# Folding a layer norm's scale and shift into the next weights, moving two norms to ScalarE, and laying the instruction order anew, in a two-layer graph transformer

## The chip, the cores and the metric

The kernel runs on one core of a Trainium2 chip. The metric is the device time of one execution in microseconds (us), the median of three runs. Inputs are 32 graphs of 512 nodes with 256 features in float32, and one 512 x 512 integer adjacency matrix for each graph.

The engines that matter here are TensorE (PE, matrix products into PSUM), its weight loads (PEld), VectorE (DVE), ScalarE (ACT), GpSimd (POOL) and the DMA queues, which are issued by SyncE (SP) and by POOL. Each engine takes its instructions strictly in the order in which the program gives them to it, and an instruction that waits for a semaphore holds up all that follow on its engine.

## The reference, cut to what matters

Each graph goes through two layers of masked attention with residuals and layer norms. `_layernorm` without arguments has no scale and shift. There are four norms for a graph; the kernel numbers them 1 to 4.

```python
def _layernorm(x, g, b):
    m = mean(x); v = mean(square(x - m))
    return (x - m) * rsqrt(v + EPS) * g + b

# layer 0
allowed = (adj > 0) | (adj.T > 0) | eye
q, k, v = split(x @ Wqkv.T + bqkv)                    # 8 heads of 32
attn    = softmax(where(allowed, q @ k.T / sqrt(32), -inf))
x1      = _layernorm(x + (attn @ v) @ Wo.T + bo, ln1_g, ln1_b)              # norm 1
ff      = relu(x1 @ W1.T + b1) @ W2.T + b2                                  # 256 -> 1024 -> 256
y       = _layernorm(x1 + ff, ln2_g, ln2_b)                                 # norm 2
x2      = _layernorm(x + y)                                                 # norm 3
# layer 1: the same attention with other weights and mask (adj != 0), no MLP
out     = _layernorm(x2 + attention(x2) @ Wo.T + bo)                        # norm 4
```

## The kernel before

All of it is a software pipeline over graphs. A class `Graph` has one small method for each step, and `period(a, b, c, d, e)` lists the steps of five graphs that are at different stages, in the order in which each engine shall execute them. `opening` (the first graphs), 29 calls of `period`, and `closing` (the last three graphs) make the whole program. This list is the schedule.

The steps that the change touches, and those that a reader needs to follow the prediction:

```python
def statistics(self, y, n, i):                    # mean and variance of one 128-row chunk
    ...
    nc.vector.bn_stats(st, y)                     # L428
    nc.vector.bn_aggr(self.mv[n][:, i, :], st)    # L429

def root(self, n, a, b):                          # rs = (var + EPS) ** -0.5, chunks a to b
    nc.gpsimd.tensor_scalar(rs, self.mv[n][:, a:b, 1:2], EPS, None, ALU.add)      # L434
    nc.gpsimd.tensor_tensor(rs, rs, neg_half[:, a:b, None], ALU.pow)              # L435

def affine(self, dst, y, g, b, n, i):             # two passes of VectorE
    nc.vector.scalar_tensor_tensor(c, y, self.mean(n, i), g, ALU.subtract, ALU.mult)             # L442
    nc.vector.scalar_tensor_tensor(dst, c, self.rs[n][:, i, :], b, ALU.mult, ALU.add)            # L443

def out0(self, i):                                # residual and statistics of norm 1
    self.residual_statistics(self.po[i // 2][:, i % 2, :], self.x1, 1, i)        # L447, 428, 429
def norm1(self, i):
    self.affine(self.x1[:, i, :], self.y.pop(i), g1, be1, 1, i)
def residual1(self):                              # x1 += b2, by an accumulating DMA
    add_row(self.x1, b2)
def norm2(self, i): ...                           # affine with g2, then statistics of norm 3
def norm3(self, i):
    nc.vector.tensor_scalar(self.x2[:, i, :], self.y.pop(i), mean, rs, ALU.subtract, ALU.mult)   # L516
def offset(self, a, b):                           # -mean * rs, for norm 4 only
    nc.vector.scalar_tensor_tensor(self.ms[:, a:b, :], self.mv[4][:, a:b, 0:1], -1.0, ...)       # L525
def norm4(self, i):
    nc.scalar.activation(self.x2[:, i, :], self.y.pop(i), AF.Identity, bias=..., scale=...)      # L530

def scores(self, layer, k):                       # one of 8 beats of a layer: 4 heads x 128 keys
    s = ps_s.tile([P, HPC, N], F32, ...)          # the only buffer of this pool (bufs=1)
    for j in range(HPC):
        nc.tensor.matmul(s[:, j, :], kT..., qT..., ...)        # L343, four row tiles of 32
    nc.scalar.activation(p, s, AF.Exp, scale=SCALE)            # L347
def masked(self, layer, k):                       # p *= mask, 128 x 2048            L352
def product(self, k):                             # acc += v.T @ p, column tiles of 32   L360
def pair(self, k):                                # p[k] += p[k+1], by a DMA of POOL     L375
def fold(self, dst, a, b):                        # p[dst] = p[a] + p[b], VectorE        L379
def sums(self, k, hg, ...):                       # ones.T @ p: softmax denominators     L400
def divide(self, hg):                             # transpose, reciprocal, transpose, multiply
def transpose(self, src, h):                      # TensorE transposes of 2 chunks       L301
def once(self):  value_bias(0)                    # first graph only: bv @ Wo + bo, needs Wo of layer 0
def once1(self): value_bias(1)                    # the same for layer 1
# project (L459), query_key (L330), value (L313), hidden (L479) and mlp (L500) are plain matmuls;
# with transpose, sums and value_bias they share ps_d, a ring of 3 PSUM buffers.
```

The loads before the loop, on the SP queue, and the last store:

```python
first.load()                                      # x of graph 0
for dst, src in resident[:5]: ...                 # Wqkv (q, k), bq, bk, Wqkv (v), bv
first.cast(); first.entries(); first.again()      # adjacency to bf16, its transposes, x again
for dst, src in resident[5:7]: ...                # Wo of layer 0, bo
second.load(); second.again()
for dst, src in resident[7:]: ...                 # W1, b1, W2, ..., Wo of layer 1, bo
...
c.store(0, 2)                                     # closing: rows of the first two chunks
c.root(4, 2, 4); c.offset(2, 4); c.norm4(2); c.norm4(3)
c.store(2, 4)
```

Of the kernel before, what the change touches and what calls it, by code (L numbers as in the profile page):

```python
# [27 lines left out]
def kernel(ctx: ExitStack, tc: tile.TileContext, t: dict, out: bass.AP):  # L28
# [15 lines left out]
    P = 128  # L44
# [49 lines left out]
    w_t, src = resident.pop()  # L94
    resident.append((w_t[:, :, : 2 * D], src[:, :, : 2 * D]))
# [8 lines left out]
    resident.insert(3, (w_t[:, :, 2 * D :], src[:, :, 2 * D :]))  # L104
# [4 lines left out]
    g1, be1 = spread("L0_gnn_ln1_g"), spread("L0_gnn_ln1_b")  # L109
    g2, be2 = spread("L0_gnn_ln2_g"), spread("L0_gnn_ln2_b")  # L110
# [11 lines left out]
    bov = [const.tile([P, D], F32, name=f"bov_{layer}") for layer in range(2)]  # L122

# [29 lines left out]
    def plain(pools: ExitStack):  # L153
# [16 lines left out]

        def add_row(dst, row):
            nc.gpsimd.dma_start(out=dst, in_=row[:, None, :].to_broadcast([P, NQ, D]), accum_op=ALU.add)
# [7 lines left out]
        class Graph:  # L180


            def __init__(self, b):
                self.b = b
                self.mv, self.rs, self.pf, self.total = {}, {}, {}, {}
# [45 lines left out]
            def once(self):  # L231

                if self.b == 0:
                    value_bias(0)

# [231 lines left out]
            def norm1(self, i):  # L467
                self.affine(self.x1[:, i, :], self.y.pop(i), g1, be1, 1, i)
# [20 lines left out]
            def residual1(self):  # L489
                add_row(self.x1, b2)  # L490
# [23 lines left out]
            def norm3(self, i):  # L514
                mean, rs = self.mean(3, i), self.rs[3][:, i, :]
                nc.vector.tensor_scalar(self.x2[:, i, :], self.y.pop(i), mean, rs, ALU.subtract, ALU.mult)  # L516
# [4 lines left out]
            def offset(self, a, b):  # L521

                if a == 0:
                    self.ms = small.tile([P, NQ, 1], F32, tag="ms", name=f"ms_{self.b}", bufs=2)
                nc.vector.scalar_tensor_tensor(  # L525
                    self.ms[:, a:b, :], self.mv[4][:, a:b, 0:1], -1.0, self.rs[4][:, a:b, :], ALU.mult, ALU.mult
                )

            def norm4(self, i):
                nc.scalar.activation(  # L530
                    self.x2[:, i, :], self.y.pop(i), AF.Identity, bias=self.ms[:, i, :], scale=self.rs[4][:, i, :]
                )

            def store(self, a=0, b=NQ):
                nc.sync.dma_start(
                    out=out[self.b].rearrange("(c p) d -> p c d", p=P)[:, a:b, :], in_=self.x2[:, a:b, :]
                )
# [4 lines left out]
        def period(a, b, c, d, e):  # L542
# [3 lines left out]
            c.scores(0, 0)  # L546
            a.fold(3, 6, 7)
            b.hidden(1, 0)
            b.hidden(1, 2)
            c.scores(0, 1)  # L550
            c.masked(0, 0)
            b.hidden(1, 4)
            b.hidden(1, 6)
            c.masked(0, 1)
            a.fold(3, 3, 4)
# [859 lines left out]
```

## Time and profile before

| | value |
|---|---|
| time, median of 3 runs | 3093.09 us (3091.61 to 3094.91) |
| busy PE, DVE, ACT, POOL, share of the span | 99%, 86%, 55%, 34% |
| mean granted TensorE clock | 0.996 |
| opening, up to the first scores of the first period | 186.7 us |
| 29 periods | 2751.1 us, 94.86 each |
| closing | 155.4 us |
| DMA traffic | 406.54 MB, 131 GB/s |

The profile comes from one execution. Its page gives busy time by engine, the span in 40 slices, the chain of work that ended last, and groups of instructions by source line with their mean duration. Answers of the trace add views of a window: the timeline of an engine, who waited for whom, and busy times by stretch. "L343" is a line of the kernel file. A count such as x16 in the trace is twice the number of matmul calls in the code, because a float32 matmul appears as two instructions. The bounds of opening, periods and closing were read from the timeline of PE: the scores that begin the first period start at 186.66 us and those that begin the closing at 2937.74 us.

### The profile page before, as it was taken

How to read it: one execution, taken by the hardware profiler on the slowest of the kernel's cores; microseconds unless marked ns; L12 is line 12 of the kernel's file. 1: busy time of each engine (PE TensorE's matmuls, PEld its weight loads, DVE VectorE, ACT ScalarE, POOL GpSimd, SP SyncE). 2: the span in 40 equal slices, each digit the busy share in tenths (PEclk: the TensorE clock that was granted, in tenths of full speed). 3: DMA queues.
4: the chain of work that ended last, by engine and by line, in shares of the span. 5: the costliest groups of instructions: out<-in, count | busy, mean ns of one | idle time of the engine just before them, and what ended most of it. 6: DMA issues, size and time to landing. Idle time of an engine off the chain costs nothing.

```text
span 3093.1 us, 44243 instructions
## 1 busy us (share of the span) xinstructions
PE 3052.6 (99%) x17218; PEld 1732.7 (56%) x17218; DVE 2648.2 (86%) x3458; ACT 1706.4 (55%) x1983; POOL 1039.8 (34%) x1254
## 2 busy tenths in 40 slices
PE   6999999999999999999999999999999999999998
PEld 2656555555555555555655555555556555555554
DVE  4798898888898888988888988889888899888887
ACT  4455655555565556655555655556555655555554
POOL 1232334332343323333333433233333334332332
PEclk8999999999999999999999999999999999999999
DMA  8776776666676666776676766668666777666542
GB/s 192 134 138 115 140 143 140 123 130 130 137 151 123 133 124 136 147 139 125 122 138 137 146 120 132 123 137 155 129 133 114 141 144 140 121 131 128 116 88 63
DMA packets 341352, 406.54 MB, mean 131 GB/s; under 512 B 149648, under 2 KB 315920, under 8 KB 316432
## 3 DMA queue, kind: packets, MB, share of 16 engines
q0 software_dynamic: 95824, 282.09, 50.8%
q1 hardware_dynamic: 245312, 121.56, 15.9%
q8 instruction: 137, 2.24, 0.3%
q14 instruction: 79, 0.65, 0.1%
HBM read 89.01 MB, written 33.55 MB: 40 GB/s over the span
## 4 chain that ended last, share of the span: by engine, by line
PE 92%; DVE 3%; DMA 2%; SPq 1%; issue 1%; ACT 1%; POOL 0%; POOLq 0%; DVEq 0%; ACTq 0%
PE psS L343 17%; PE psH L479 15%; PE psF L500 14%; PE psA L360 14%; PE psQK_None L330 10%; PE psV L313 7%; PE psO L459 7%; PE psR L400 4%; PE psQK L330 3%; PE psT L301 2%; DVE p L352 1%; DMA p<-p 1%; DMA v<-in_x_dram 1%; DMA s_L_gnn_ln_g<-in_L_gnn_ln_g_dram 0%; ACT p L347 0%
## 5 line engine op out<-in xcount | busy, mean ns | idle before, releaser
L347 ACT ACTIVATE p<-psS 128x2048 f32<-128x2048 f32 x512 | 961.8, 1879 | 652.9 <-PE psS L343 647.4
L352 DVE TENSOR_TENSOR p<-p,m 128x2048 f32<-128x2048 f32 x512 | 1155.3, 2279 | 30.3 <-ACT p L347 30.3
L434 POOL TENSOR_SCALAR rs<-mv 128x2 f32<-128x2 f32 (+1 forms) x320 | 321.7, 1005 | 935.6 <-DVE mv L429 933.6
L343 PE MATMUL psS<-qT,kT 32*128 32x512 f32 x4096 | 585.6, 641 | 8.0 <-ACT p L347 6.2
L360 PE MATMUL psA<-p,v 128*32 128x512 f32 x4096 | 491.9, 598 | 0.9 <-ACT cT L370 0.7
L500 PE MATMUL psF<-w_L_gnn_W,hT 128*128 128x256 f32 x2048 | 469.1, 383 | 0.0
L479 PE MATMUL psH<-xT,w_L_gnn_W 128*128 128x256 f32 x2048 | 467.4, 384 | 0.0
L500 PEld LDWEIGHTS psF<-w_L_gnn_W,hT 128*128 128x128 f32 x2048 | 384.5, 190 | 124.2 <-issue 77.6
L479 PEld LDWEIGHTS psH<-xT,w_L_gnn_W 128*128 128x128 f32 x2048 | 382.2, 190 | 117.5 <-issue 44.7
L379 DVE TENSOR_TENSOR p<-p,p 128x2048 f32<-128x2048 f32 x189 | 429.2, 2286 | 2.6 <-DMA p<-p 2.4
L343 PEld LDWEIGHTS psS<-qT,kT 32*128 32x128 f32 x4096 | 160.6, 184 | 305.2 <-issue 114.3
L435 POOL TENSOR_TENSOR rs<-rs,neg_half 128x2 f32<-128x2 f32 (+1 forms) x320 | 304.8, 952 | 26.8
L360 PEld LDWEIGHTS psA<-p,v 128*32 128x32 f32 x4096 | 110.2, 109 | 315.3 <-issue 233.8
L487 ACT ACTIVATE hT<-psH,c_L_gnn_b 128x256 f32<-128x256 f32 x512 | 214.8, 471 | 123.3 <-PE psH L479 119.9
L415 POOL TENSOR_TENSOR total<-total,sT 128x16 f32<-128x16 f32 x128 | 28.4, 222 | 732.7 <-DVE sT L412 732.7
L459 PE MATMUL psO<-w_L_gnn_Wo,cT 128*128 128x256 f32 x1024 | 241.2, 383 | 0.9 <-DVE cT L419 0.9
L330 PE MATMUL psQK_None<-xT,w_L_gnn_Wqkv 128*128 128x512 f32 x512 | 237.8, 598 | 2.2 <-ACT xT L289 1.6
L375 POOL DMA_DIRECT2D p<-p x189 | 186.9, 991 | 141.3 <-PE psA L360 81.0
L370 ACT COPY cT<-psA 128x512 f32<-128x512 f32 x128 | 74.9, 585 | 278.6 <-PE psA L360 278.6
L447 DVE TENSOR_TENSOR y<-psF,x 128x256 f32<-128x256 f32 x128 | 53.9, 421 | 195.9 <-PE psF L500 188.9
L459 PEld LDWEIGHTS psO<-w_L_gnn_Wo,cT 128*128 128x128 f32 x1024 | 189.5, 190 | 51.5 <-DVE cT L419 22.2
L428 DVE BATCH_NORM_STATS2 st<-y 128x6 f32<-128x256 f32 x384 | 164.3, 428 | 13.1
(68 smaller groups left out, 2938.0 us busy)
## 6 DMA issues: line engine op xcount, KB each, us to landing
p<-p POOLq DMA_DIRECT2D x189, 1024.0 KB, 7.7
x<-in_x_dram SPq DMA_DIRECT2D x64, 512.0 KB, 5.1
x<-bov POOLq DMA_DIRECT2D x64, 512.0 KB, 9.1
code<-in_adj_dram POOLq DMA_DIRECT2D x32, 512.0 KB, 6.4
m<-code SPq DMA_DIRECT2D x32, 512.0 KB, 5.6
x<-s_L_gnn_ln_b POOLq DMA_DIRECT2D x32, 512.0 KB, 10.4
x<-s_L_gnn_b POOLq DMA_DIRECT2D x32, 512.0 KB, 5.5
kT<-v SPq DMA_DIRECT2D x248, 64.0 KB, 3.4
```

Source lines behind the costliest of these rows:

```text
L313: nc.tensor.matmul(ps[:, j, :], self.xT[:, i, at], proj[layer][0][2][:, i, :], start=(i == 0), stop=(i == ND - 1),)
L330: nc.tensor.matmul(ps, w[:, i, c * P : (c + 1) * P], self.xT[:, i, at], start=(i == 0), stop=(i == ND - 1))
L343: nc.tensor.matmul(s[:, j, :], self.kT[at, hg, kc * P : (kc + 1) * P], self.qT[at, hg, :], start=True, stop=True)
L347: nc.scalar.activation(p, s, AF.Exp, scale=SCALE)
L352: nc.vector.tensor_tensor(p, p, m[:, k % NQ, None, :].to_broadcast([P, HPC, N]), ALU.mult)
L360: nc.tensor.matmul(self.acc[hg][j * HD : (j + 1) * HD, :], self.v[:, kc, h * HD : (h + 1) * HD], self.p[k][:, j, :], start=(kc == 0), stop ...
L379: nc.vector.tensor_tensor(self.p[dst], self.p[a], self.p[b], ALU.add)
L434: nc.gpsimd.tensor_scalar(rs, self.mv[n][:, a:b, 1:2], EPS, None, ALU.add)
L435: nc.gpsimd.tensor_tensor(rs, rs, neg_half[:, a:b, None], ALU.pow)
L459: nc.tensor.matmul(ps[:, j, :], self.cT[:, k, at], wo[layer][:, k, :], start=(k == 0), stop=(k == ND - 1))
L479: nc.tensor.matmul(ps[:, j, :], w1[:, c, at], self.xT[:, c, h * 2 * P : (h + 1) * 2 * P], start=(c == 0), stop=(c == ND - 1),)
L500: nc.tensor.matmul(ps, self.hT[h][:, f, j * P : (j + 1) * P], w2[:, f, :], start=(f == 0), stop=(f == NF - 1))
```

## The change: what it does and what it is for

Norm 1 without its scale and shift is kept in x1 for the MLP: `relu(W1 (g1 * n + be1) + b1)` equals `relu((W1 g1) n + (W1 be1 + b1))`, so g1 goes into W1 once, on the chip, and W1 be1 into b1 (`fold_norm1`, called by `once2` for the first graph). The residual of norm 2 still needs `g1 * n + be1 + b2`; `residual1` makes it with one VectorE multiply over the whole graph and the accumulating DMA that was there before, whose row is now be1 + b2. With that, norm 1 has the plain form of norms 3 and 4, and all three become `y * rs + (-mean * rs)`: one small VectorE instruction for -mean * rs and one ScalarE activation for each chunk. It is meant to take load from VectorE. The order lists of `opening`, `period` and `closing` are all new. Two things of the kernel before are absent: Wqkv is one load again, and the last graph is stored in one piece, after all four chunks.

```diff
-    w_t, src = resident.pop()
-    resident.append((w_t[:, :, : 2 * D], src[:, :, : 2 * D]))
-    resident.insert(3, (w_t[:, :, 2 * D :], src[:, :, 2 * D :]))
+    g1_c, be1_c = column("L0_gnn_ln1_g"), column("L0_gnn_ln1_b")
+    row12 = const.tile([P, D], F32, name="row12")
...
+        def fold_norm1():
+            ps = ps_d.tile([P, NF], F32, tag="d", name="psW_0")
+            for f in range(NF):
+                for c in range(ND):
+                    nc.tensor.matmul(ps[:, f : f + 1], w1[:, c, f * P : (f + 1) * P], be1_c[:, c : c + 1], ...)
+            nc.vector.tensor_tensor(b1, b1, ps, ALU.add)
+            for c in range(ND):
+                nc.vector.tensor_scalar(w1[:, c, :], w1[:, c, :], g1_c[:, c : c + 1], None, ALU.mult)
+            nc.vector.tensor_tensor(row12, be1, b2, ALU.add)
...
             def norm1(self, i):
-                self.affine(self.x1[:, i, :], self.y.pop(i), g1, be1, 1, i)
+                self.shifted(1, self.x1, i)
             def residual1(self):
-                add_row(self.x1, b2)
+                nc.vector.tensor_tensor(self.x1, self.x1, g1[:, None, :].to_broadcast([P, NQ, D]), ALU.mult)
+                add_row(self.x1, row12)
             def norm3(self, i):
-                nc.vector.tensor_scalar(self.x2[:, i, :], self.y.pop(i), mean, rs, ALU.subtract, ALU.mult)
+                self.shifted(3, self.x2, i)
-            def offset(self, a, b):
+            def offset(self, n, a, b):
+            def shifted(self, n, dst, i):
+                bias, scale = self.ms[n][:, i, :], self.rs[n][:, i, :]
+                nc.scalar.activation(dst[:, i, :], self.y.pop(i), AF.Identity, bias=bias, scale=scale)
-            def store(self, a=0, b=NQ):
+            def store(self):
...
         def opening(a, b, c, d):          # start of the new list; all cut but the head
             a.flip(0, 0)
             a.join(0, 0)
             a.join(0, 1)
-            a.masks()
+            a.once()
             a.query_key(0, 0, 0)
             a.query_key(0, 1, 0)
+            a.value(0, 0)
+            a.masks()
             a.scores(0, 0)
...
```

In the old `opening`, `once1` stood ahead of `scores(0, 6)` of the first graph, `once` ahead of `scores(0, 7)`, and the `join` steps of the second graph (ScalarE copies of transposed input) ahead of `scores(0, 5)` and after `scores(0, 7)`. In the new one `once` is the first matmul step after the input transposes, both joins follow `scores(0, 7)`, `once2` comes after the first graph's attention, and `once1` stands late in the opening.

The part of the new `period` around norm 1 of graph c, which the prediction walks through (the engine of each step is added):

```python
c.sums(3, 1, ...)      # PE
c.divide(1)            # DVE
b.masked(1, 1)         # DVE
b.scores(1, 3)         # PE, then exp on ACT
b.query_key(1, 0, 1)   # PE
c.project(0, 0)        # PE
b.scores(1, 2)         # PE, then exp on ACT
c.project(0, 1)        # PE
c.out0(0); c.out0(1)   # DVE
a.offset(4, 2, 4)      # DVE
c.root(1, 0, 2)        # POOL
c.offset(1, 0, 2)      # DVE
b.masked(1, 0)         # DVE
c.norm1(1); c.norm1(0) # ACT
b.value(1, 1)          # PE
b.masked(1, 2)         # DVE
c.transpose(c.x1, 0)   # PE
```

In the old `period`, `project(0, 0)` and `project(0, 1)` were followed by two beats of scores and three products before the transpose of x1.

The end of the new `closing` is `c.root(4, 2, 4)`, two offsets, four `c.norm4`, `b.store()`, `c.store()`.

## The prediction, made before the changed kernel was run

> **What bounds the kernel now.** I read the page's first part, then the busy times of three stretches (opening, 29 periods, closing), then what PE waited for.
>
> ```profile
> PE 3052.6 (99%) x17218; PEld 1732.7 (56%) x17218; DVE 2648.2 (86%) x3458; ACT 1706.4 (55%) x1983; POOL 1039.8 (34%) x1254
> ```
>
> ```profile
> core 0: us, PE busy (x) PEld busy (x) DVE busy (x) ACT busy (x) POOL busy (x), PEclk, DMA share, GB/s
> 0.00:187.00 187.00, 159.02 (x820) 87.55 (x824) 118.84 (x146) 84.61 (x96) 40.13 (x58) 0.94 0.74 154
> 187.00:2938.00 2751.00, 2749.97 (x15548) 1564.84 (x15544) 2402.47 (x3134) 1544.38 (x1798) 955.33 (x1130) 1.00 0.68 133
> 2938.00:3093.00 155.00, 143.66 (x858) 80.34 (x854) 126.88 (x180) 77.45 (x89) 44.39 (x66) 0.99 0.39 76
> ```
>
> In 2751 us of periods PE idles 1.03 us in all. "Busy" could hide slow matmuls, so I listed PE's timeline of one period and took the distance from each group's start to the next: sixteen 256-column matmuls take 3.45 us between other full-array matmuls and 3.65 us between two score groups. A score group always takes 1.07, a product group 0.88 to 0.99. So each change between score, product and full-array groups costs about 0.1 us on either side, and the rest is streaming. **The periods are bound by PE's work, not by VectorE**, busy 87% there. Only the 28 us idle in the opening and the 11 in the closing are waits:
>
> ```profile
> PE psB L166 <- DMA w_L_gnn_Wo<-in_L_gnn_Wo_dram: 12.8, 1, 12.8
> PE psS L343 <- ACT p L347: 6.2, 1, 6.2
> ```
>
> The columns are total, times and longest. The first is `once1` waiting for the last weights; the second a score group behind an exp behind joins that waited for their DMA (ScalarE idle 19.3 us).
>
> **What the Trainium skill says.** "VectorE: DVE Perf Modes", section "The perf-mode tier table", gives 2293 ns for a float32 tensor_tensor of 2048 elements; the masks here take 2279. "SBUF — State Buffer", section "SBUF: two separate sides", says VectorE and GpSimd share a port pair under an exclusive lock, also when VectorE reads two SBUF inputs. The trace agrees; first POOL's timeline, then VectorE's (start, duration):
>
> ```profile
> 1005.16 0.36 POOL L434 TENSOR_SCALAR rs<-mv 128x2 f32<-128x2 f32 x1 [4.92 <-DVE mv L429]
> 1009.98 2.15 POOL L434 TENSOR_SCALAR rs<-mv 128x2 f32<-128x2 f32 x1 [2.77 <-DVE mv L429]
> ```
>
> ```profile
> 1009.80 2.26 DVE L352 TENSOR_TENSOR p<-p,m 128x2048 f32<-128x2048 f32 x1
> ```
>
> The same `root` instruction takes 0.36 us alone and 2.15 under a mask. "TensorE: Matmul & The Clock Gate", section "Part 1: The HAM clock gate", says that the array runs slower after idling; the first eight 512-column projections took 5.29 us, later eight 3.70.
>
> **The change, part by part.** Rows by shape:
>
> ```profile
> L442 DVE SCALAR_TENSOR_TENSOR cent<-y,mv,s_L_gnn_ln_g 128x256 f32<-128x256 f32 x256 | 119.5, 467 | 2.5
> L443 DVE SCALAR_TENSOR_TENSOR x<-cent,rs,s_L_gnn_ln_b 128x256 f32<-128x256 f32 x128 | 62.1, 485 | 35.9 <-POOL rs L435 30.4
> L516 DVE TENSOR_SCALAR x<-z,mv,rs 128x256 f32<-128x256 f32 x128 | 48.9, 404 | 36.7 <-POOL rs L435 36.7
> L525 DVE SCALAR_TENSOR_TENSOR ms<-mv,rs 128x2 f32<-128x2 f32 x64 | 9.8, 153 | 1.2 <-POOL rs L435 1.1
> L530 ACT ACTIVATE x<-y,ms,rs 128x256 f32<-128x256 f32 x128 | 70.1, 600 | 9.5 <-DVE ms L525 9.5
> ```
>
> (Busy total, mean ns, idle before.) *VectorE, per graph*: out go four norm 1 (119.5/2 + 62.1 = 121.9 us over 32 graphs, 3.8 each) and four norm 3 (48.9/32 = 1.5); in come five more offsets (5 x 0.15 = 0.8) and the multiply in `residual1` (1024 elements, half a mask: 1.1). Net -3.4 of some 83 us. *ScalarE*: eight more activations at 0.55 (70.1/128): +4.4 on 53. *PE*: nothing per graph. Neither engine bounds the periods, so the offload as such is worth 0.
>
> *The new period order.* Old and new lists have the same 70 matmul groups and, counted in both, the same 37 changes of kind; with the group costs above both sum to within 0.1 us. Score beats are never closer than 3.4 us in the new list, and one buffer of scores allows 3.14 (closest starts in the trace, 16.59 and 19.73). So 94.8 us stays the floor, and **the new order can only add waits**. The tightest chain I find is norm 1's, from the end of `sums(3, 1)` to the transpose of x1. PE's work between: scores 1.07, projection of q or k 1.81, project 1.82, scores 1.07, project 1.82, value 1.73 = 9.32 us. The chain: PE to VectorE 0.20 (1030.21 to 1030.41), `divide` 2.46, mask 2.20, two `out0` 2.00, `root` 1.38 (1004.98 to 1006.36), offset and handover 0.23, two activations 1.09, handover 0.07 = 9.63 us. That is 0.3 us late per period. The old order gave this chain two score beats and three products more. Second: `fold(2, 2, 0)` waits for `pair(2)`, whose transfer lands 7 to 9.7 us after issue, and the denominators of the layer come 10.8 us after the product that allows the issue, of which the fold takes 2.2: 0 to 0.3 us late. I choose 0.35 us per period: 29 x 0.35 = **+10 us**, plausible from 0 to 25.
>
> *Opening.* Wo of layer 0 is issued at 14.60 us, behind the adjacency transposes, and such a load lands in 3.4 to 4.3 us; `once` now waits for it before the first projection, which before started at 7.38. Away go the waits of 12.8 and 6.2. First scores come at about 18.9 + 2.05 (`value_bias`) + 5.3 (cold projections) + 2.0 (value) = 28.2, before 13.45; seven more at 3.14 and some 1 us for masks put the eighth at 51, before 57.4. But then exp and four joins (2.8 us) stand ahead of the second graph's value, a fold and a mask ahead of the last product, and `fold_norm1` adds 16 matmul calls of one column, 32 weight loads at 0.19 us: 6.1. The next graph's first scores, at 69.22 before, come at 75 without further waits and at 78 with 3 us for fold and divide, while 4.7 us of work (a sum, a projection, a project) has moved ahead of them: +4. Later the transpose of x2 has about 2 us too little cover. **Opening +6, from -4 to +12.** One Wqkv load instead of two: the q and k half was not what the first projection waited for (it started 0.05 us after ScalarE's copy), so 0 to +1, hidden behind `once`.
>
> *Closing.* 63 changes of kind against 58: +1. Norms 2 and 3 of the last graph's second half have about 6.5 us between the MLP's end and the transpose, with 5.2 of PE work: +1.3. At the end four activations instead of two follow the last offset (+1.1), and one 512 KB store ends where a 256 KB one did (those land in 2.3 us): about +1. **Together +4**, from 2 to 7.
>
> Sum: 3093 + 10 + 6 + 4 = **3113 us**, 0.6% slower.
>
> **Rivals.** (1) *VectorE's relief pays.* For: 86% busy, the second engine. Against: PE idles 1 us in 2751. It would need PE to wait for VectorE now; the trace has one such wait of 0.7 us. The time would then be 3093 plus the edges, some 3095 to 3103; the same holds if the new order simply fits. (2) *A new wait in each period*: ScalarE is handed norms between exps, and an offset makes VectorE wait for POOL. For: my sum of 0.3 us, and the port lock, which can turn a `root` of 1.1 us into 3. If one root falls under a mask (2.2 us more) ahead of a transpose, the periods give 29 x 1.9 = 55 us more: 3150 to 3165. (3) *The opening gains*: the 19 us of waits vanish and the transfers of `pair` no longer collide with weight loads, so that weights land sooner. Against: `once` puts a wait of the same size at the front. It would make 3080 to 3090 if the periods fit.
>
> **Range and chances.** The edges leave -4 to +19, the periods 0 to 25. They are not at their ends together, so 8 in 10 lie in 3092 to 3142. More than 2% faster (3031) would need PE's work to shrink: 1%. Within 2%: 93%. Slower than 3155 needs 1.5 us of waits per period, rival 2: 6%.
>
> **What will show it.** PE's groups with unchanged totals (scores 585 us, MLP 467 and 469). Periods of 95.0 to 95.3 instead of 94.86, with PE waiting for ScalarE before the transpose of x1 as the most frequent wait. VectorE near 2540 us, ScalarE near 1850. In the opening a wait of PE for Wo of 11 to 12 us near 7, 16 calls of `fold_norm1` near 6 us, and the 12.8 gone; the end about 2 us longer after the last projection. Periods of 96 or more, or an opening below 183 us, would make me wrong.

## The result, and the profile after

The changed kernel takes 3134.83 us (median of four runs, 3132.30 to 3139.34), beside 3093.89 us of the kernel before on the same chip: 1.0135 times as long, with a 95% interval of 1.0117 to 1.0153. It is 41 us slower where 20 were predicted: inside the range of 3092 to 3142, and twice the predicted loss. The page's first line of the kernel after:

```profile
PE 3070.0 (98%) x17250; PEld 1731.0 (55%) x17250; DVE 2566.1 (82%) x3270; ACT 1828.2 (58%) x2239; POOL 940.1 (30%) x1254
```

VectorE has less to do and ScalarE more, as meant, and PE has the same work, but for the folding at the start, with more time around it. The busy times of opening, periods and closing, cut at the first scores of the first period (192.49 us) and of the closing (2973.50 us):

```profile
core 0: us, PE busy (x) PEld busy (x) DVE busy (x) ACT busy (x) POOL busy (x), PEclk, DMA share, GB/s
0.00:192.50 192.50, 164.33 (x850) 92.16 (x850) 116.78 (x145) 90.66 (x110) 44.42 (x63) 0.97 0.71 145
192.50:2973.50 2781.00, 2760.33 (x15549) 1559.06 (x15545) 2327.93 (x2958) 1655.24 (x2028) 854.04 (x1129) 1.00 0.68 132
2973.50:3130.00 156.50, 145.32 (x862) 79.78 (x858) 121.43 (x169) 82.25 (x101) 41.69 (x64) 0.98 0.38 75
```

The 29 periods grew from 2751.1 to 2781.0 us (+30), the opening from 186.7 to 192.5 (+6), the closing from 155.4 to 157.0 (+2). PE, which idled 1 us in all periods of before, now idles 21; the other 10 us lie in what the profile counts as busy, as short waits or slower work, which this view doesn't tell apart. What it waited for in the periods of after (columns: total, times, longest):

```profile
PE psR L420 <- DVE p L399: 7.1, 8, 1.3
PE psR L420 <- DVE sT L432: 5.9, 5, 1.7
PE psT L321 <- ACT x L552: 4.4, 15, 0.4
PE psR L420 <- ACT hT L508: 2.5, 4, 0.6
```

The first line is `sums` waiting for a `fold`. The second is the second `sums`, whose PSUM buffer is freed by a `divide` that stands behind a fold. The third is the norm 1 chain that I had expected to lead: it is the most frequent wait, 15 times, and costs 4.4 us in all. VectorE's own waits in the periods say where the folds lose their time, first after, then before:

```profile
DVE y L467 <- PE psF L522: 39.2, 29, 1.4
DVE p L399 <- DMA p<-p: 30.5, 37, 2.8
```

```profile
DVE y L447 <- PE psF L500: 187.6, 58, 4.1
DVE p L379 <- DMA p<-p: 1.7, 4, 1.1
```

A fold (L399, before L379) waits for the additive transfer of a `pair`: 30.5 us where it was 1.7. Before, VectorE had 187.6 us in which it stood waiting for the MLP's product; in after 39.2 are left, although it has less work. The room went to other places of the order, not to the end of these waits.

Two periods of after on GpSimd and VectorE (start, duration). The transfers into p[2] and p[4] of layer 0 are issued by the L395 lines; the folds are the L399 lines. First a period without loss, then one of the longest:

```profile
223.94 0.92 POOL L395 DMA_DIRECT2D p<-p  x1 [0.35 <-PE psA L380]
226.86 0.86 POOL L395 DMA_DIRECT2D p<-p  x1 [2.00 <-DVE st L448]
231.40 4.49 DVE L399 TENSOR_TENSOR p<-p,p 128x2048 f32<-128x2048 f32 x2
236.18 2.29 DVE L399 TENSOR_TENSOR p<-p,p 128x2048 f32<-128x2048 f32 x1 [0.30 <-DMA p<-p]
...
703.66 0.92 POOL L395 DMA_DIRECT2D p<-p  x1 [0.35 <-PE psA L380]
706.58 0.85 POOL L395 DMA_DIRECT2D p<-p  x1 [2.00 <-DVE st L448]
711.12 4.49 DVE L399 TENSOR_TENSOR p<-p,p 128x2048 f32<-128x2048 f32 x2
718.27 2.29 DVE L399 TENSOR_TENSOR p<-p,p 128x2048 f32<-128x2048 f32 x1 [2.66 <-DMA p<-p]
```

In both the fold of p[2] comes 7.46 us after its transfer was issued, and VectorE is ready for the fold of p[4] 9.0 us after that one was issued (226.86 + 9.0 = 235.9). It then waits 0.3 us in the first period and 2.66 in the second. The old order issued the two 4.4 us apart and came to the folds 9.4 and 9.5 us later.

The transfer into p[2] itself is hardly slower than before: it lands 7.0 to 7.7 us after issue in 24 periods of before and 8.2 to 8.6 in the other five, 7.0 to 7.4 in 22 periods of after and 8.4 to 9.2 in seven. The fold at 9.4 came after all of these, the fold at 7.46 comes ahead of the late ones. The transfer into p[4] takes 8.2 us at best in before and 9.1 in after, where it follows sooner. And the loss of a period is the fold's wait: in the five periods in which the fold of p[4] waits longest (1.72, 1.77, 2.37, 2.66 and 2.76 us) the period is 1.47, 1.52, 2.13, 2.41 and 2.51 us longer than a clean one of 95.01.

How late the periods are is best read from the starts of the score groups on PE. A clean period of after takes 95.01 us, of before 94.78; the means are 95.90 and 94.87. Of the 0.9 us that a mean period of after stands above a clean one, most lies in the score distances that hold `sums` and what follows them.

### The profile page after: what moved, and what is told of

Same layout as the page of the kernel before. It is cut to its first block, busy times and chain, and to the rows that moved or that the text cites. A ratio compares the mean times of both kernels' runs of the same rounds, so it can differ in the third digit from the quotient of the medians.

```text
span 3130.5 us, 44346 instructions
## 1 busy us (share of the span) xinstructions
PE 3070.0 (98%) x17250; PEld 1731.0 (55%) x17250; DVE 2566.1 (82%) x3270; ACT 1828.2 (58%) x2239; POOL 940.1 (30%) x1254
## 5 line engine op out<-in xcount | busy, mean ns | idle before, releaser
L380 PE MATMUL psA<-p,v 128*32 128x512 f32 x4096 | 499.5, 598 | 1.9 <-DVE p L372 1.0
L454 POOL TENSOR_SCALAR rs<-mv 128x2 f32<-128x2 f32 (+1 forms) x320 | 258.4, 808 | 727.0 <-DVE mv L449 601.9
L399 DVE TENSOR_TENSOR p<-p,p 128x2048 f32<-128x2048 f32 x189 | 430.0, 2288 | 41.3 <-DMA p<-p 36.3
L395 POOL DMA_DIRECT2D p<-p x189 | 173.1, 916 | 476.8 <-PE psA L380 367.4
L455 POOL TENSOR_TENSOR rs<-rs,neg_half 128x2 f32<-128x2 f32 (+1 forms) x320 | 274.0, 856 | 26.7
L479 PE MATMUL psO<-w_L_gnn_Wo,cT 128*128 128x256 f32 x1024 | 251.6, 388 | 1.4 <-DVE cT L439 0.9
L479 PEld LDWEIGHTS psO<-w_L_gnn_Wo,cT 128*128 128x128 f32 x1024 | 187.1, 191 | 90.1 <-issue 39.2
L435 POOL TENSOR_TENSOR total<-total,sT 128x16 f32<-128x16 f32 x128 | 38.5, 301 | 655.8 <-DVE sT L432 653.4
L508 ACT ACTIVATE hT<-psH,c_L_gnn_b 128x256 f32<-128x256 f32 x512 | 206.9, 470 | 45.0 <-PE psH L500 44.4
L552 ACT ACTIVATE x<-y,ms,rs 128x256 f32<-128x256 f32 x256 | 148.8, 595 | 62.9 <-DVE ms L546 57.1
L432 DVE STREAM_TRANSPOSE sT<-psR 128x512 f32<-128x512 f32 x128 | 91.2, 713 | 112.3 <-PE psR L420 109.5
```

The source lines that it names most:

```text
L380: nc.tensor.matmul(self.acc[hg][j * HD : (j + 1) * HD, :], self.v[:, kc, h * HD : (h + 1) * HD], self.p[k][:, j, :], start=(kc == 0), stop ...
L399: nc.vector.tensor_tensor(self.p[dst], self.p[a], self.p[b], ALU.add)
L479: nc.tensor.matmul(ps[:, j, :], self.cT[:, k, at], wo[layer][:, k, :], start=(k == 0), stop=(k == ND - 1))
L508: nc.scalar.activation(self.hT[h][:, f + j, :], ps[:, j, :], AF.Relu, bias=b1[:, f + j : f + j + 1])
```

## The experiments

In the table, "period" is the mean of the 29 periods in the profiled run and "start" the time at which the first one begins. The opening of after, unchanged, began the periods at 192.5 to 198.2 us in seven of these kernels, so I compare periods where only they were changed. Each ratio is to runs of before on the same chip, whose medians were 3093.06 to 3093.89.

| kernel | median us | ratio to before (95%) | period us | start us |
|---|---|---|---|---|
| before | 3093.89 | 1 | 94.87 | 186.7 |
| after | 3134.83 | 1.0135 (1.0117 to 1.0153) | 95.90 | 192.5 |
| e1 no transfers | 3102.53 | 1.0029 (1.0018 to 1.0041) | 95.02 | 189.3 |
| e2 late transpose | 3137.51 | 1.0144 (1.0128 to 1.0161) | 95.89 | 198.2 |
| e3 late sums | 3139.84 | 1.0151 (1.0134 to 1.0168) | 96.02 | 197.0 |
| e4 old order, new norms | 3150.24 | 1.0188 (1.0171 to 1.0205) | 95.94 | 205.4 |
| e5 new order, old norms | 3239.15 | 1.0470 (1.0453 to 1.0488) | 99.10 | 193.3 |
| e6 late `once` | 3148.47 | 1.0175 (1.0158 to 1.0192) | 95.91 | 207.8 |
| e7 without p[2] += p[3] | 3110.39 | 1.0048 (1.0032 to 1.0065) | 95.16 | 194.9 |
| e8 early p[0] += p[1] | 3149.63 | 1.0181 (1.0164 to 1.0198) | 96.37 | 193.2 |
| e9 before, late p[2] += p[3] | 3105.01 | 1.0038 (1.0025 to 1.0050) | 95.34 | 186.1 |
| e10 e2 and masks swapped | 3134.55 | 1.0134 (1.0117 to 1.0150) | 95.85 | 195.8 |
| e11 combined | 3137.99 | 1.0142 (1.0125 to 1.0159) | 96.06 | 194.6 |
| e12 before, x first | 3092.07 | 0.9996 (0.9987 to 1.0005) | 94.87 | 183.7 |
| e13 e12, residual later | 3089.97 | 0.9990 (0.9982 to 0.9998) | 94.88 | 181.3 |
| e14 room for transfers | 3154.31 | 1.0195 (1.0179 to 1.0211) | 96.50 | 196.6 |
| e15 without bias transfers | 3129.7 (one run) | | 95.94 | 188.9 |
| e16 e13, residual split | 3087.80 | 0.9983 (0.9975 to 0.9991) | 94.88 | 179.0 |
| e17 room, second try | 3259.90 | 1.0536 (1.0520 to 1.0552) | 100.20 | 193.9 |

**e1: no additive transfers.** Theory: the transfers come late for the folds. Rival: the norm 1 chain with its offset and ScalarE.

```diff
 def pair(self, k):
-    if not self.final():
-        nc.gpsimd.dma_start(out=self.p[k], in_=self.p[k + 1], accum_op=ALU.add)
+    return
```

> The kernel after without the three additive transfers of each graph and layer (p[0] += p[1], p[2] += p[3], p[4] += p[5]); it leaves out three of eight terms of the softmax denominators, everything else stays. Theory A (the transfers land late, so that fold, sums and divide stall PE): the waits of PE for folds and sums go, with them some 18 us of the 26 us of uneven score distances; periods near 95.2 us in place of 95.90, total 3110 to 3120. Theory B (the norm 1 chain with its root, offset and ScalarE activations, or the port lock, makes the loss): the time stays within 5 us of the 3134.8 of after. Under both the norm 1 chain still costs about 0.35 us per period.

Measured 3102.53 us. All that PE still waited for in the periods of e1:

```profile
PE psT L321 <- ACT x L551: 0.3, 1, 0.3
```

The periods fell to 95.02 us, between 95.00 and 95.36. So the transfers make (95.90 - 95.02) x 29 = 25 us of the 30. The waits for the norm 1 chain went with them, 4.4 to 0.3 us: that chain was late only because VectorE was. The gain is larger than I expected; such followers are part of it. What is left against before, 0.16 us a period, is no wait that a record shows.

**e2 and e10: the norm 1 chain.** e2 moves the transpose of x1 behind the next score group; e10 also swaps two masks, so that the first product after it does not need the one behind norm 1's offset.

```diff
-            c.transpose(c.x1, 0)
             b.scores(1, 4)
+            c.transpose(c.x1, 0)
```

```diff
             c.divide(1)
-            b.masked(1, 1)
+            b.masked(1, 0)
...
             c.offset(1, 0, 2)
-            b.masked(1, 0)
+            b.masked(1, 1)
```

> The kernel after with the transpose of x1's first half in each period moved behind the next score group (one swap of two groups, same work). Theory: the norm 1 chain is 0.3 to 0.4 us late in nearly every period, and this gives it 1.07 us more: the distance from score group (1,2) to (1,4) loses the wait, some 11 us in all, total 3122 to 3126. If the chain is not what PE waits for there, or the wait only moves on to hidden(0, 0): 3132 to 3137.

> The kernel after with the transpose of x1's first half one score group later, as tried already, and the masks of beats 0 and 1 of layer 1 swapped, so that product 0 no longer waits for the mask behind norm 1's offset. If the steady 0.2 us and the 5 us of uneven distances ahead of this transpose are VectorE's chain, which the first try only moved on to product 0: 6 to 11 us less than after, 3124 to 3129. If they are something else: 3133 to 3138.

In neither did the expected gain come: periods of 95.89 and 95.85 against 95.90. In e2 the shortest distance between the score groups around the transpose fell from 5.33 to 4.72 and the next one rose from 3.78 to 4.40, the same sum. The 0.6 us is the price of the transposing itself, which moved with it, and not a wait. The uneven 5 us moved on too, to products that wait for masks (2.6 us in e2, 2.4 in e10). Giving this chain more time is worth nothing, since it is not what starts late.

**e3: folds and sums loosened.**

```diff
-            c.fold(2, 2, 0)
+            c.fold(3, 6, 7)
             b.query_key(1, 1, 1)
             b.scores(1, 0)
-            c.fold(3, 6, 7)
+            c.fold(2, 2, 0)
             ...
-            c.sums(2, 0, first=True, last=True)
             c.product(7)
-            c.divide(0)
             b.scores(1, 1)
             b.query_key(1, 1, 0, 1)
+            c.sums(2, 0, first=True, last=True)
+            c.divide(0)
```

> The kernel after with more time between the transfers and what needs them, same work: fold(3, 6, 7), which needs no transfer, goes ahead of fold(2, 2, 0), and sums(2, 0) with its divide go 2.9 us of PE work later. Theory A (late landings): the stalls at product 6, sums(2, 0) and product 7 go, half of those at sums(3, 1): 10 to 17 us less, total 3118 to 3125. Theory B: no gain, or a few us slower since divide(0) comes later and pushes the norm 1 chain: 3133 to 3150.

Measured 3139.84: no gain, though the stalls did shrink. Above their minima, the three distances that hold these sums lost 17.7 us over all periods in after and 7.8 in e3. But the minima themselves rose by 0.55 us a period, 16 us in all: the next score group now follows after 3.14 us, the least that one buffer of scores allows, and sums stand between full-array groups. The new places cost more than the stalls that they saved. And the swap of the folds gave the first transfer no room: fold(3, 6, 7) needs no transfer's result, but it writes p[3], which the transfer p[2] += p[3] still reads, so it has to wait for the same landing. VectorE still waited 25.5 us for transfers in these periods.

**e4: the old order with the new norms**, each offset just ahead of the first norm that needs it.

```diff
             c.root(1, 0, 2)
-            c.norm1(0)                        # two passes of VectorE
+            c.offset(1, 0, 2)                 # VectorE
+            c.norm1(0)                        # ScalarE; all other norms 1 and 3 alike
```

> The kernel before, its order and its loads, with only the arithmetic of the change: norms 1 and 3 on ScalarE, each offset put just ahead of the first norm that needs it, W1 and b1 folded in the opening. If the offload as such is worth nothing and the new order makes the loss: 3094 to 3102, of which 3.5 us are the folding of b1. If offset, ScalarE and POOL make the loss whatever the order: 3110 to 3140. If VectorE's relief pays: below 3090.

Measured 3150.24, above the whole range that I gave. The periods are 1.07 us longer, nearly all by the same amount, and start 19 us later. ScalarE's waits for its norms in the periods of e4, then PE's:

```profile
ACT x L555 <- DVE ms L549: 153.8, 58, 8.9
```

```profile
PE psV L336 <- ACT xT L312: 9.2, 29, 0.7
PE psS L366 <- ACT p L370: 8.4, 29, 3.4
```

ScalarE stands up to 8.9 us in front of a norm whose offset is not there yet, and the exps and copies behind it come late. The sum of these waits is not what tells: in after it is 171.2 us, but there the longest is 4.3 us, and PE waits only 4.4 us behind them. VectorE's relief bought nothing here: the norms cost PE a wait where ScalarE met them too early. What the relief would bring without this wait, e4 doesn't show.

**e5: the new order with the old norms.**

```diff
 def norm1(self, i):
-    self.shifted(1, self.x1, i)
+    self.affine(self.x1[:, i, :], self.y.pop(i), g1, be1, 1, i)
 def offset(self, n, a, b):
+    if n != 4: return
```

> The kernel after, its order and loads, with the arithmetic of before: norms 1 and 3 on VectorE with their affine parts, no folding, no offsets but norm 4's. If the new order alone makes the loss (its three additive transfers stand within 10.1 us), the stalls at fold and sums stay, total 3130 to 3145. If the loss needs the offload (offsets, ScalarE), it comes near before: 3095 to 3115. VectorE has 3.4 us more per graph to do than in after, so some more waits are to be expected from it: 3140 to 3160 is possible too.

Measured 3239.15, above all three ranges. PE's largest wait in its periods:

```profile
PE psT L320 <- DVE x L462: 72.9, 29, 2.7
```

It waits in every period, up to 2.7 us, for VectorE's norm 1. So the new order needs the offload: each alone loses, 57 us (e4, of which 31 lie in the periods and 19 in the opening) and 146 us (e5); together 41.

**e6: the opening's `once` behind the fifth score group.**

```diff
-            a.once()
             a.query_key(0, 0, 0)
             ...
             a.scores(0, 4)
+            a.once()
```

> The kernel after with the opening's once (PE multiplying the value bias by Wo, which waits 12.7 us for its weights) moved from the front to behind the fifth score group. If that wait is what the opening of after pays: the first scores come 11 to 13 us sooner, and the periods start 6 to 10 us sooner, 3125 to 3129. If the second graph's x, joined at 53.7 us, is what sets the end of the opening: the periods start 0 to 4 us sooner, 3131 to 3135.

Both expectations missed: 3148.47, the periods start 15 us later. The wait for Wo went and the eighth scores came at 40.2 us in place of 50.7, but then:

```profile
PE psV L333 <- ACT xT L309: 33.8, 1, 33.8
```

PE stood 33.8 us for the second graph's x, until 76.2 us, where after had it at 55.1. With everything 10 us sooner, the first graph's additive transfers (the first issued at 29.7 us in place of 40.8) were under way together with the loads that x stands behind. The last of these in the stretch from 20 to 76 us, first in after, then in e6 (size, time to landing):

```profile
w_L_gnn_Wo<-in_L_gnn_Wo_dram SPq DMA_DIRECT2D x1, 256.0 KB, 3.3
```

```profile
w_L_gnn_Wo<-in_L_gnn_Wo_dram SPq DMA_DIRECT2D x1, 256.0 KB, 28.3
```

It took 28.3 us in place of 3.3, and the queue issued x's first transposing load at 52.7 us in place of 33.7. That the transfers held these loads up is read from their times alone; no run took them out of this opening. And PE came back slower: the value projection after the pause took 3.78 us against 1.89 before it, in a stretch (40 to 80 us) in which the trace shows a mean granted clock of 0.57. That is what the Trainium skill says ("TensorE: Matmul & The Clock Gate", section "Part 1: The HAM clock gate") of an array that has idled.

**e7 and e8: which transfer is one too many?** e7 leaves out p[2] += p[3] of layer 0; e8 issues the first transfer of layer 0 4.8 us sooner.

```diff
-    if not self.final():
+    if not self.final() and (self.layer, k) != (0, 2):
```

```diff
             c.scores(0, 3)
+            c.product(0)
...
-            c.product(0)
...
             a.project(1, 0)
+            c.pair(0)
...
-            c.pair(0)
```

> The kernel after with one of the three additive transfers of layer 0 left out (p[2] += p[3]; one of eight terms of the denominators is missing). If transfers stand in line behind each other (7.2 and 2.9 us apart at about 5.6 us of transfer time each), the other two have room and the stalls go as they did without any transfer: periods 95.0 to 95.1, total 3104 to 3112. If a landing varies by itself (7 to 11.7 us whatever its neighbours), the stalls at the fold that waits for p[4] stay: periods 95.4 or more, total 3117 to 3128.

> The kernel after, same work, with product 0 and the first additive transfer of layer 0 issued some 5 us earlier in each period, so that it has landed when the second is issued. If the line of three transfers makes the stalls: the fold that waits for p[2] no longer stalls, the one that waits for p[4] by 0.5 us at most, periods 95.1 to 95.3, total 3110 to 3118. If the two transfers that stay 2.9 us apart are enough to make it: periods 95.5 to 95.8, 3123 to 3132.

e7 came in nearly as expected, 3110.39 with periods of 95.16 for 95.0 to 95.1: in all its periods one fold of layer 0 waited, 0.2 us. What is left are six waits of the first fold of layer 1, 0.6 to 1.4 us, which after has too. e8 missed: with 12.6 us between the first and the second transfer the folds waited in nearly the same periods, VectorE for transfers 23.7 us against 30.5 and PE for folds 10.0 against 7.1, and the early product made clean periods 0.5 us longer. So the first of the three transfers is not what makes the loss. It takes the two that follow each other within 2.9 us.

**e9: the loss made in the kernel before.**

```diff
-            c.pair(2)
             a.root(4, 0, 2)
+            c.pair(2)
             c.pair(4)
```

> The kernel before, one swap in the period: the additive transfer into p[2] is issued behind norm 4's root instead of ahead of it, so some 3.9 us later and about 1 us ahead of the one into p[4], while the folds stay where they are. If two transfers of 1 MB need 10.4 us of all the engines whatever the order of the rest, the fold of p[2] waits 1.5 to 2.5 us in every period and the fold of p[4] some more, and PE waits for sums by 0.5 to 2 us per period: 3108 to 3150. If only the new order's surroundings make the landings late, the folds wait 0.5 us at most: 3093 to 3098.

Measured 3105.01, 11.5 us slower than before, with periods of 95.34. VectorE's waits for transfers in the periods of e9:

```profile
DVE p L379 <- DMA p<-p: 12.9, 14, 2.2
```

They were 1.7 us in before. I had the direction, and the size too high: the root held the transfer up by 1.3 us and not 3.9, so the two were 3.1 us apart, with 8.0 and 9.5 us to their folds. The transfer into p[4] now lands after 9.3 us at best in place of 8.2, which leaves its fold no margin in the old order either, and folds stall in about half of the periods, as in after.

**e14 and e17: room for the transfers, all work done.** e14 puts fold(3, 6, 7) first, a mask ahead of the last fold, both sums behind one more score group and the projection behind a value group. e17 moves one mask and one product of e14 again.

```diff
-            c.fold(2, 2, 0)
+            c.fold(3, 6, 7)
...
+            b.masked(1, 0)
             c.fold(3, 3, 4)
...
             b.scores(1, 3)
+            c.sums(2, 0, first=True, last=True)
+            c.divide(0)
             c.sums(3, 1, first=True, last=True)
...
+            b.value(1, 1)
             c.project(0, 0)
```

```diff
+            b.masked(1, 2)
             c.offset(1, 0, 2)
-            b.masked(1, 2)
...
+            b.product(2)
             c.transpose(c.x1, 0)
-            b.product(2)
```

> The kernel after, same work and the same number of changes of kind on PE, with room for the two transfers: the fold that needs none goes first, the mask of beat (1, 0) stands ahead of the fold that waits for p[4], both sums stand behind score group (1, 3), the projection behind value(1, 1), the transpose of x1 behind product 1. The fold of p[2] then comes 9.7 us after its transfer's issue in place of 7.5, that of p[4] 11.2 in place of 9.0. If the loss in the periods is the transfers' lateness alone: periods 95.2 to 95.6, total 3110 to 3125. If the norm 1 chain, now with less cover, takes over: 3125 to 3150.

> The kernel after with room for the transfers, second try: the mask of beat (1, 2) ahead of norm 1's offset, product 2 ahead of the transpose of x1, since in the first try product 2 waited 0.4 us for that mask in every period. The stalls of PE for folds and sums should stay as small as in the first try (2 us in all, after has 14). If the mask was the rest of the cost: periods 95.4 to 95.9, 3120 to 3137. If the norm 1 chain takes the place of the mask: 96.2 or more, 3145 or more.

Measured 3154.31 and 3259.90. PE's waits in the periods of e14:

```profile
PE psA L380 <- DVE p L372: 12.1, 29, 0.4
PE psS L363 <- ACT kT L353: 9.0, 12, 1.3
PE psR L420 <- DVE p L399: 1.4, 5, 0.3
```

The waits for folds and sums are gone but for 1.4 us, as meant, and a mask and a copy of ScalarE have taken their place. But the first transfer got no room here either, since fold(3, 6, 7) overwrites what it reads. The issue into p[2] and the first fold in period 11 of e14, counted from 0:

```profile
1290.95 0.92 POOL L395 DMA_DIRECT2D p<-p  x1 [0.34 <-PE psA L380]
1300.30 4.50 DVE L399 TENSOR_TENSOR p<-p,p 128x2048 f32<-128x2048 f32 x2 [1.80 <-DMA p<-p]
```

VectorE was ready 7.55 us after the issue (1300.30 - 1.80 - 1290.95), as in after, and waited for the landing, though this fold is not the one of p[2]. Only the fold of p[4] had its room. A fold of 6 and 7 into p[6] or p[7] would leave p[3] alone; no run tried that. In e17 one mask of 2.3 us stands ahead of norm 1's offset; ScalarE waits 312 us for offsets in its periods (254 in e14, 171 in after), what stands behind them is late, and the period is 4.3 us longer than in after. No full computation in the new order has won the 25 us back. That the order can't give the room is not shown; three tries, e3 and these two, had the same flaw in the first fold.

**e15: the rhythm of the late landings.** The two bias transfers per graph are left out.

```diff
 def residual(self):
-    add_row(self.x1, bov[0])
-    add_row(self.x, be2)
+    return
```

> The kernel after without the two additive bias transfers per graph (512 KB each, of bov into x1 and of the second norm's shift into x; both are left out of the result). They have landed long before the stalls. In after the fold of p[2] is 0.9 to 1.8 us late in periods 1, 6, 11, 15, 20, 24 and 25, the fold of p[4] 1.7 to 2.8 us in periods 5, 10, 14, 19 and 28. If this rhythm follows the number of transfers issued so far in that queue (10 per period, now 8): the late periods become other ones, further apart (every 5.8 instead of 4.7 periods). If it follows something else, such as the fetching of instructions or the place of the buffers: the same periods are late as in after. The time should stay near that of after, 3120 to 3137.

Counted from 0, the same periods are late: the fold of p[4] by 1.7 us or more in 5, 10, 14, 19 and 28, the fold of p[2] mostly in 6, 11, 15, 20 and 24. The count of transfers in the queue is not what sets the rhythm. The other branch, the fetching of instructions, is taken up in the last section.

**e11, e12, e13, e16: the opening.** What comes out of e6 is that x of the second graph has to be loaded ahead of the weights. e12 does that to the kernel before, and e13 and e16 remove what then held the first graph up. e11 does it to after, together with e2, e10 and an earlier value group.

```diff
+            second.flip(0, 0); second.flip(0, 1); second.sort(0, 0); second.sort(0, 1)
             second.load()
...         # opening
-            b.flip(0, 0) ... b.sort(0, 1)
-            a.once1()                         # now among the MLP products of the first graph
-            b.residual()                      # e13: now behind a.divide(1)
+            a.residual_x()                    # e16: its second transfer too, behind a.divide(1)
```

> The kernel after, same work: once behind the fifth score group; the second graph's x (its transposing loads and their sorting) ahead of the weights in the queue of loads; in each period value(1, 0) of the next layer ahead of its first score group, the late transpose and the swapped masks. Expected if the wait for x and the lateness of VectorE behind the transfers are the causes: periods start 15 to 20 us sooner than in after, at 173 to 178 us, and are 95.2 to 95.6 long: 3098 to 3112. If the waits only move on: 3118 to 3132.

> The kernel before with a new opening order alone: the second graph's x ahead of the weights in the queue of loads, and once1 (which waited 12.8 us for the last weights) much later. If these two waits of the opening (19 us of PE) can be taken away: periods start 12 to 20 us sooner, 3073 to 3082, faster than both kernels. If the weights and transfers that come later then hold up the first MLP: 3083 to 3096.

> The kernel before with the opening's new order of loads (second graph's x first, once1 late), and now also the additive bias transfers of the second graph behind the first graph's divides, since in the last try GpSimd waited 11.9 us in its queue for the loads that these transfers need, and the divide behind it. If that was the only wait the new loads made: the first graph's projection comes 8 to 11 us sooner, 3081 to 3087, faster than both kernels. If the weights of the MLP then arrive too late, or VectorE is the next limit: 3086 to 3093.

> The last opening on the order and arithmetic of before, with the first graph's second bias transfer (of norm 2's shift, whose load arrives at 59 us) split off and put behind the divides too: GpSimd waited 17.9 us for that load and held the divide up by 8.7 us. If that was the rest of the wait: the first projection comes 6 to 8 us sooner, 3082 to 3086, faster than before by its interval. If the next thing (weights of the MLP, masks of the second graph) takes over: 3086 to 3091.

In e12 the second graph's first scores came at 48.5 us in place of 69.2, but the periods began only 3 us sooner. VectorE in e12:

```profile
64.48 0.71 DVE L418 STREAM_TRANSPOSE rT<-r 128x512 f32<-128x512 f32 x1 [11.92 <-POOL total L415]
```

The divide waited 11.9 us for a small sum on GpSimd. That queue stood before bias transfers whose data were not loaded yet (in e13 still 17.9 us for one of them). e13 and e16 took two of these transfers out of the way: 3.8 and 5.9 us less than before. e16 is the best kernel of the study, 3087.80 us, faster than both (0.9983, 0.9975 to 0.9991). Of the 28 us that PE idled in the opening 20 are still idle: the next wait is 7.0 us for norm 1. e11 met the wait of the divide for GpSimd as well (11.1 us), so that its periods began at 194.6 us and not at 173 to 178, and they kept their loss: 3137.99, no gain.

## Why the prediction was wrong, and where it was right

**What bounds the kernel: held.** In e1, with VectorE relieved and no late transfer, the periods are flat at PE's pace and no shorter than before. VectorE's removed and added rows net -108 us; 3.4 x 32 = 109 were predicted. Its busy time, which counts overlapping instructions once, fell by 82, to 2566 us and not to 2540; ScalarE's rose to 1828, for 1850.

**The floor: slightly off.** "The same" work on PE takes 95.01 us in a clean period and not 94.78. With it, the periods of e1 stand 0.16 us above those of before on average: 4.6 us in all. Which groups pay isn't settled. I had allowed 0.1 us in the sum, and it is 0.23.

**The failed step: the size of the second chain, and with it the +10 us for the periods, which measured +30, beyond my 0 to 25.** The prediction put 0 to 0.3 us on the path from the transfer into p[2] to the denominators, and 0.3 us on norm 1's chain, "the tightest chain I find". It is the other way round. The transfers cost 0.87 us a period (e1), norm 1's chain nothing by itself (e2, e10, and its wait gone in e1). Two things were mis-sized. I reckoned with the transfer into p[2] alone, and the one into p[4], 2.9 us behind it, lands 9.1 to 11.7 us after issue for a fold that VectorE is ready for at 9.0. And I took landings of 7 to 9.7 us as a spread to be averaged, where each late one counts in full, since there was hardly a margin under it: 7.5 us to the first fold, where the old order gave 9.4. The data was there, in the issue times of the two orders. A period of 96 us or more "would make me wrong", I wrote; it was 95.90 on average and up to 97.5.

**The opening: right in the sum** (+5.8 for +6), by parts that I had mostly sized well: first scores at 28.55 for 28.2, eighth at 50.70 for 51. `fold_norm1` took 3.5 us, not 6.1, and the next graph's scores came at 80.50, not 78. The wait for Wo is 12.7 us, for 11 to 12. What was wrong is its meaning: I treated it as loss, and in e6 the opening without it is 15 us longer. Since the same opening gave starts from 192.5 to 198.2, the agreement is partly luck, and the rest of the 41 us (the two profiled runs differ by 37) lies there or in the spread of the runs.

**The closing: +1.6 for +4**, just below its range.

**The rivals.** The first, that VectorE's relief pays, did not show: the time is 32 us above its 3103. It also named what comes if the new order simply fits, 3095 to 3103, and e1, without the transfers, is there with 3102.53. The third, an opening that gains because transfers no longer collide with weights, is refuted for this change. The second, a new wait in each period, was the right family with the wrong member: neither the root nor the port lock, but the landing of two transfers.

## What to carry to other kernels

When an order is laid anew, list for each transfer the time from issue to first use in the old and the new order, and hold it against the latest landing, not the usual one; what was hidden with 2 us to spare is not hidden with none. Count as a use also the instruction that overwrites what a transfer reads. Before believing a tightest chain, take away what feeds it: a wait at the end of a chain often belongs to its start. An offload to an engine that works in order needs its inputs ready when the engine gets there (e4), so it and the order are one change and are judged together.

## What the runs showed of the hardware that I had not expected

**Two transfers of 1 MB need 10.4 us of all sixteen DMA engines.** The bytes moved in 16 us from shortly before the first issue, in 40 slices, in a period of after without loss, with the row of the queue:

```profile
GB/s 0 0 0 102 225 328 0 328 266 61 328 205 123 328 0 328 328 0 328 205 123 328 61 266 328 0 328 328 0 0 0 0 0 0 163 215 222 148 74 241
q0 software_dynamic: 288, 2.10, 65.1%
```

65.1% of 16 us is 10.4 us, 5.2 for each transfer. A packet is counted in the slice in which it starts; the last of these start in the slice that ends 11.2 us into the window. The Trainium skill ("DMA: Bandwidth & Descriptors", section "Anatomy of one DMA — SWDGE (gpsimd) path") gives a fit of 2.0 us and the bytes at 436 GB/s; for 1 MB my estimate from it is 4.4 us for the whole transfer. These transfers, which add into SBUF, landed in 7.0 us at best and are slower than that; here the measurement decides.

**In a late landing one of sixteen completions is late, and an instruction packet stands beside it.** The same view of the period that lost 2.66 us, with the row of a queue that the view of the clean period doesn't have:

```profile
GB/s 0 0 0 143 184 328 20 307 287 41 328 266 61 328 0 328 307 20 328 287 41 328 184 143 328 61 266 307 20 0 41 0 0 0 148 209 243 125 59 215
q8 instruction: 1, 0.02, 0.4%
```

All but one packet of the transfers start as early as in the clean period. The slice of 20 GB/s is the last one, of 8 KB; the slice of 41 GB/s, 16 KB, is the packet of the instruction queue. Each transfer ends with sixteen completion packets of 4 bytes. For the one into p[4] fifteen are done at 11.8 us of the window and the last at 13.15, when the instruction packet ends (13.17); in the clean period all are done at 11.8. The fold starts 1.5 us after that last one and in the clean period 0.4, so some 1 us of the 2.66 stays open.

I compared this in all 29 periods of after. In 13 one of the sixteen completions, of p[4]'s transfer or of both, comes 0.6 to 1.7 us behind the others. In 12 of these a packet of q8 starts 5.9 to 12.2 us after the issue into p[2] and before the last completion. In the other 16 none starts there: it comes within 1 us of the issue, or with or behind the last completion. The exception is period 25, with such a packet 0.8 us after the issue. Packets of q8 come every 22.5 us on average, so that they meet the two transfers in some periods only. That fits the rhythm, and e15, where the same periods are late. In before, completions 1.3 to 1.7 us late occur as well; nearly all folds come after them. No run moved or removed these packets, so that they make the landings late is argued, not shown.
